# Expert tiles that join the block pipeline of the feed-forward part, from three tables

## The chip, the cores and the metric

The kernel runs on one core of a Trainium2 chip. Its time is device microseconds of that core. In the profile, PE is TensorE's matrix multiply and PEld its weight load, DVE is VectorE, ACT is ScalarE, POOL is GpSimd, and SP is SyncE, which issues most loads. All arithmetic is in 32-bit floats unless noted.

## The reference, cut to what matters

The layer works on x of 8 sequences of 512 tokens with 256 features. It has windowed causal self-attention with 16 heads, then cross-attention to 64 context rows per sequence, then a feed-forward part. The change is in the feed-forward part only, which is (with S = 512 positions and B = 8 sequences in the role of the batch):

```
xn  = layer_norm(x)
y   = layer_norm1(attention over the 8 sequences of a position(xn) + xn)
idx = argmax(y @ Wg.T)                       # one of E = 8 experts for each of 4096 tokens
for e in range(E):
    h   = relu(y @ W1[e] + b1[e])            # 256 -> 1024
    out = out + (idx == e) * (h @ W2[e] + b2[e])   # 1024 -> 256
result = x + layer_norm2(y + out)
```

The reference computes all experts for all tokens and masks. The kernel sorts the tokens by expert and computes for each only its own.

## The kernel before, in words

There are three stages. The first (lines 194 to 690) does both attentions, sequence by sequence; its output goes to a DRAM tensor x2d. The change does not touch it.

**The block stage** (lines 702 to 954). The 4096 tokens are split into NBLK = 8 blocks of 512 (64 positions x 8 sequences), each of NG = 4 groups of 128. For a block n there are a load (`block_load`, SyncE, into a buffer y that holds for each token two times 256 numbers and its token number), `block_start` (layer norm, transposes on PE, products for queries, keys and values), four `group` works (scores with a mask, maxima on DVE, exponentials on ACT, reciprocal on DVE, scaling of the softmax weights s by it on POOL at line 826, transposes on PE at line 831, product with the values at 838, output product at line 849), and a `block_end` (layer norm on DVE with a power on POOL, transposes at line 862, router product at line 868, arg max, the running count of tokens per expert `seens`, the rank of each token within its expert, and four scatters at line 928). A scatter is an indirect DMA on POOL's queue which writes 128 rows of 513 numbers to the DRAM tensor rows_d. Row e * 4096 + rank belongs to the token with that rank in expert e.

**The table** (lines 968 to 1025). When all 8 blocks are counted, a product with ones gives the number of tokens of each expert, and some twenty small DVE instructions make from them, for each of NT = 39 tiles: its expert (`eidx`), the row of rows_d for each of its 128 partitions (`srci`), and which of them are empty (`void`). 39 is the most that 4096 tokens in 8 experts can need when each expert's last tile may be partly filled.

**The tile stage** (lines 1027 to 1105). `expert_tile(i)` goes over six steps: SyncE reads the expert number and issues the loads of W1 (1 MB), b1 and b2, and POOL gathers the tile's rows from rows_d (line 1039); a step of nothing; transposes on PE (1055); 16 products of the hidden layer (1066, the profile counts two instructions for each) with the ReLU on ACT (1072) and DVE (1074); 8 products with W2 (1081, all of W2 lies in SBUF) and the layer norm's statistics (1084 to 1091); the norm's end and a scatter to the output (1095).

**What sets the order.** `in_steps` runs works as generators. A work has a start step; in each step every active work runs up to its next `yield`, in the order of its rank (PREFIX first, EXPS last), and among equals the latest begun first:

```
PREFIX, TURN, VALUES, SMALL, SCORES, OTHER, EXPS = range(7)
...
works.append((4 * n, block_start(n)))
for g in range(NG):
    works.append((4 * n + 6 + g, group(n, g)))
```

So block n's groups begin at steps 4n + 6 to 4n + 9, and its `block_end` at step 4n + 15, with scatters five and six steps later. `in_order` then fixes that order on PE, DVE, ACT and POOL: none of them may pass an instruction that waits. SyncE's queue is placed by the framework's scheduler. The framework also adds waits where a buffer is used again and where one DMA reads what another has written. For rows_d, the scatters are declared disjoint among themselves.

The tile stage is a second call of `in_steps`, with pools of its own (`ws`, `tp`, `mo`, `ps_f`, `ps_m3`), opened after the block stage's pools are closed.

Of the kernel before, what the change touches and what calls it, by code (L numbers as in the profile page):

```python
# [8 lines left out]
F32 = mybir.dt.float32  # L9
I32 = mybir.dt.int32  # L10
# [7 lines left out]
P = 128  # L18
# [8 lines left out]
NG = 4  # L27
# [5 lines left out]
NT = (B * S + E * (P - 1)) // P  # L33
ROW = 2 * D + 1
# [3 lines left out]
PREFIX, TURN, VALUES, SMALL, SCORES, OTHER, EXPS = range(7)  # L38
# [58 lines left out]
def decoder_kernel(ctx: ExitStack, tc: tile.TileContext, a: dict, out: bass.AP):  # L97
# [604 lines left out]
    with ExitStack() as p2:  # L702
# [5 lines left out]
        fy = p2.enter_context(tc.tile_pool(name="fy", bufs=7))  # L708
        state = [{} for _ in range(NBLK)]

        def block_load(n):

            state[n]["yr"] = yr = fy.tile([P, NG, ROW], F32, tag="y", name=f"y_{n}")
            for g in range(NG):
                p0 = (n * NG + g) * GP
                nc.sync.dma_start(yr[:, g, D : 2 * D], x2d[:, p0 : p0 + GP, :])
# [21 lines left out]
        def block_start(n):  # L738
# [21 lines left out]
            for hf in range(2):  # L760
# [7 lines left out]
                k = fx.tile([P, 512], F32, tag="k", bufs=4)  # L768
# [172 lines left out]

        block_load(1)
        works = [(9, expert_weights())]
        for n in range(NBLK):
            works.append((4 * n, block_start(n)))
            for g in range(NG):
                works.append((4 * n + 6 + g, group(n, g)))
            if n < NBLK - 1:
                works.append((4 * n + 15, block_end(n, 0, NG)))
            else:  # L950
                works.append((4 * n + 13, block_end(n, 0, NG // 2)))
                works.append((4 * n + 15, block_end(n, NG // 2, NG // 2)))
        with in_order(tc):
            in_steps(works)
    seen = seens[-1]

    ps_f = ctx.enter_context(tc.tile_pool(name="ps_f", bufs=4, space=PSUM))
    ps_m = ctx.enter_context(tc.tile_pool(name="ps_m3", bufs=4, space=PSUM))
    ws = ctx.enter_context(tc.tile_pool(name="ws", bufs=4))
    tp = ctx.enter_context(tc.tile_pool(name="tp", bufs=1))  # L960
    mo = ctx.enter_context(tc.tile_pool(name="mo", bufs=2))
    tb = []
    for i in range(7):
        tb.append(tp.tile([P, ROW], F32, name=f"tb{i}"))
        nc.gpsimd.memset(tb[i], 0.0)


    pn = ps_m.tile([P, E], F32, tag="m")
    nc.tensor.matmul(pn, ones, seen, start=True, stop=True)
    cnt = wp.tile([P, E], F32, name="cnt")  # L970
    nc.vector.tensor_copy(cnt, pn)

    def by_pairs(n, m, name):
        return wp.tile([P, n, m], F32, name=name)

    t8 = by_pairs(E, NGRP, "t8")
    nc.vector.tensor_tensor(
        t8,
        cnt.unsqueeze(2).to_broadcast([P, E, NGRP]),
        cst[:, C_128 : C_128 + NGRP].unsqueeze(1).to_broadcast([P, E, NGRP]),  # L980
        ALU.is_gt,
    )
    nt = wp.tile([P, E], F32, name="nt")
    nc.vector.tensor_reduce(nt, t8, AX.X, ALU.add)
    sc = by_pairs(E, E, "sc")
    nc.vector.tensor_tensor(
        sc,
        nt.unsqueeze(1).to_broadcast([P, E, E]),
        cst[:, C_SCAN : C_SCAN + E * E].rearrange("p (a b) -> p a b", b=E),
        ALU.mult,  # L990
    )
    first = wp.tile([P, E], F32, name="first")
    nc.vector.tensor_reduce(first, sc, AX.X, ALU.add)

    tiles = cst[:, C_TILE : C_TILE + NT].unsqueeze(2).to_broadcast([P, NT, E])
    begun = by_pairs(NT, E, "begun")
    nc.vector.tensor_tensor(begun, tiles, first.unsqueeze(1).to_broadcast([P, NT, E]), ALU.is_ge)
    ei = wp.tile([P, NT], F32, name="ei")
    nc.vector.tensor_reduce(ei, begun, AX.X, ALU.add)
    eidx = wp.tile([P, NT], I32, name="eidx")  # L1000
    nc.vector.tensor_scalar(eidx, ei, -1.0, None, ALU.add)


    oe = wp.tile([P, 2, 1 + E], F32, name="oe")
    nc.gpsimd.memset(oe, 0.0)
    nc.vector.scalar_tensor_tensor(
        oe[:, 0, 1:], first, -float(P), cst[:, C_E4 : C_E4 + E], ALU.mult, ALU.add
    )
    nc.vector.scalar_tensor_tensor(oe[:, 1, 1:], first, float(P), cnt, ALU.mult, ALU.add)
    od = wp.tile([P, 2, E], F32, name="od")  # L1010
    nc.vector.tensor_tensor(od, oe[:, :, 1:], oe[:, :, :E], ALU.subtract)
    ob = wp.tile([P, 2, NT, E], F32, name="ob")
    ov = wp.tile([P, 2, NT], F32, name="ov")
    for i in range(2):
        nc.vector.tensor_tensor(
            ob[:, i], begun, od[:, i].unsqueeze(1).to_broadcast([P, NT, E]), ALU.mult
        )
    nc.vector.tensor_reduce(ov, ob, AX.X, ALU.add)
    pos = cst[:, C_POS : C_POS + NT]
    void = wp.tile([P, NT], F32, name="void")  # L1020
    nc.vector.tensor_tensor(void, pos, ov[:, 1], ALU.is_ge)
    src = wp.tile([P, NT], F32, name="src")
    nc.vector.tensor_tensor(src, ov[:, 0], pos, ALU.add)
    srci = wp.tile([P, NT], I32, name="srci")
    nc.vector.scalar_tensor_tensor(srci, void, float(FAR), src, ALU.mult, ALU.add)

    def expert_tile(i):

        e_sp = nc.sync.value_load(eidx[0:1, i : i + 1], min_val=0, max_val=E - 1)
# [179 lines left out]
```

## Time and profile before

| | us |
|---|---|
| three runs | 1229.08, 1237.77, 1235.94 |
| median of the runs | 1235.94 |
| the profiled execution, its own time | 1234.02 |
| its span, from the first to the last instruction | 1232.3 |
| PE busy in the span | 1098.1 (89%) |
| PE's weight loads busy | 792.0 (64%) |
| DVE busy | 713.4 (58%) |
| ACT busy | 581.2 (47%) |
| POOL busy | 501.1 (41%) |
| first PE product of the block stage | 678.2 |
| last PE product of the block stage and table | 908.8 |
| first hidden layer of the tile stage | 932.5 |
| last PE product | 1217.4 |

The times of single instructions below come from the profiled execution and count from its span's start. A group's line has the source line, engine, operation, output<-input by tile name, how often, and busy time. In a timeline line the first number is the start, the second the duration, both in us, and the bracket at the end says how long the engine was idle before it and what released it. The granted clock is the share of full speed that PE was given. Matmuls are pipelined, so pieces of PE's timeline overlap by about 0.1 us.

### The profile page before, as it was taken

How to read it: one execution, taken by the hardware profiler on the slowest of the kernel's cores; microseconds unless marked ns; L12 is line 12 of the kernel's file. 1: busy time of each engine (PE TensorE's matmuls, PEld its weight loads, DVE VectorE, ACT ScalarE, POOL GpSimd, SP SyncE). 2: the span in 40 equal slices, each digit the busy share in tenths (PEclk: the TensorE clock that was granted, in tenths of full speed). 3: DMA queues.
4: the chain of work that ended last, by engine and by line, in shares of the span. 5: the costliest groups of instructions: out<-in, count | busy, mean ns of one | idle time of the engine just before them, and what ended most of it. 6: DMA issues, size and time to landing. Idle time of an engine off the chain costs nothing.

```text
span 1232.3 us, 24539 instructions
## 1 busy us (share of the span) xinstructions
PE 1098.1 (89%) x8901; PEld 792.0 (64%) x8901; DVE 713.4 (58%) x1804; ACT 581.2 (47%) x2040; POOL 501.1 (41%) x578
## 2 busy tenths in 40 slices
PE   6798998999989998998973999999737999999995
PEld 3455666566655665656542566676527999999994
DVE  2947768486684857857542436765652454545453
ACT  2866659576586766768510465555401111111110
POOL 2242424314343233522410333454353555555553
PEclk9997999999999999999997899999867999999998
DMA  5000001010010101000003840111066566666630
GB/s 190 1 1 5 6 1 45 1 39 6 18 27 2 44 1 36 10 1 27 2 18 98 242 131 2 52 53 52 35 170 243 196 206 218 223 208 208 217 126 9
DMA packets 60727, 97.66 MB, mean 79 GB/s; under 512 B 15930, under 2 KB 43965, under 8 KB 60608
## 3 DMA queue, kind: packets, MB, share of 16 engines
q1 hardware_dynamic: 53056, 75.08, 19.3%
q0 software_dynamic: 7552, 21.02, 5.0%
q8 instruction: 72, 1.18, 0.4%
q14 instruction: 47, 0.39, 0.1%
HBM read 81.12 MB, written 17.71 MB: 80 GB/s over the span
## 4 chain that ended last, share of the span: by engine, by line
PE 70%; DVE 15%; ACT 5%; issue 3%; POOL 3%; DMA 2%; SPq 0%; POOLq 0%; DVEq 0%
PE ps L183 12%; PE ps L1066 12%; PE ps L188 11%; PE ps L1081 11%; ACT s L447 3%; DVE nm L443 2%; PE sc L400 2%; DVE s L427 2%; PE xav L634 2%; DVE nm L576 2%; PE pt L476 2%; PE ps L802 2%; PE ps L177 2%; PE xk L598 2%; PE av L505 1%
## 5 line engine op out<-in xcount | busy, mean ns | idle before, releaser
L447 ACT ACTIVATE s<-s,nm 128x144 f32<-128x144 f32 (+1 forms) x512 | 203.4, 408 | 10.9 <-DVE nm L443 10.9
L1072 ACT ACTIVATE h<-ps,b 128x128 f32<-128x128 f32 x156 | 44.5, 368 | 261.3 <-issue 225.8
L1066 PE MATMUL ps<-tT,w 128*128 128x128 f32 x1248 | 148.3, 278 | 1.7 <-DMA b<-in_b 1.7
L1066 PEld LDWEIGHTS ps<-tT,w 128*128 128x128 f32 x1248 | 145.0, 195 | 2.1 <-issue 2.1
L1081 PE MATMUL ps<-w,h 128*128 x624 | 141.0, 379 | 0.0
L482 POOL TENSOR_TENSOR pc<-pT,cst 128x512 f32<-128x512 f32 x96 | 123.2, 1304 | 25.8 <-DVE pT L478 25.4
L1081 PEld LDWEIGHTS ps<-w,h 128*128 128x128 f32 x624 | 115.8, 191 | 14.0
L447 ACT ACTIVATION_READ_ACCUMULATOR s<-s,nm 128x1 f32 x512 | 100.8, 197 | 0.0
L458 POOL COPY rx<-s 128x128 f32<-128x128 f32 x48 | 14.6, 305 | 192.6 <-ACT s L447 192.6
L443 DVE TENSOR_REDUCE nm<-s 128x8 f32<-128x1152 f32 (+1 forms) x64 | 84.5, 1320 | 13.2 <-POOL s L436 9.4
L400 PE MATMUL sc<-kz,qT 32*128 32x512 f32 (+1 forms) x512 | 76.0, 603 | 4.1 <-DVE s L419 3.0
L427 DVE COPY_PREDICATED s<-upto_q,sc 128x512 f32<-128x512 int32 x96 | 64.6, 726 | 24.6 <-ACT s L426 24.6
L476 PE MATMUL pt<-cst,s 128*128 128x128 f32 x512 | 72.6, 282 | 2.6 <-ACT pT L480 1.1
L1074 DVE TENSOR_SCALAR h<-ps,b 128x128 f32<-128x128 f32 x156 | 43.9, 344 | 51.8 <-ACT h L1072 40.7
L156 POOL TENSOR_TENSOR rs<-rs,nhalf 128x4 f32<-128x4 f32 (+1 forms) x33 | 33.7, 1021 | 95.1 <-DVE rs L155 94.8
L476 PEld LDWEIGHTS pt<-cst,s 128*128 128x128 f32 x512 | 60.4, 145 | 15.5 <-issue 7.2
L426 ACT COPY s<-sc 128x512 f32<-128x512 f32 x96 | 51.6, 590 | 38.3 <-PE sc L400 38.3
L1091 POOL TENSOR_TENSOR rs<-rs,nhalf 128x1 f32<-128x1 f32 x39 | 26.5, 680 | 106.1 <-DVE rs L1090 91.3
L1084 DVE TENSOR_TENSOR r<-ps,r 128x256 f32<-128x256 f32 x39 | 16.6, 425 | 90.1 <-PE ps L1081 87.8
L183 PE MATMUL ps<-fxT,w_fwqkv 128*128 128x512 f32 x128 | 60.9, 621 | 0.0
L826 POOL TENSOR_TENSOR s<-s,sm 128x512 f32<-128x512 f32 x32 | 33.3, 1042 | 65.3 <-DVE sm L825 65.1
L461 DVE RECIPROCAL rc<-sm 128x8 f32<-128x8 f32 x64 | 12.6, 197 | 80.0 <-ACT s L447 80.0
(198 smaller groups left out, 2341.3 us busy)
## 6 DMA issues: line engine op xcount, KB each, us to landing
w<-in_W SPq DMA_DIRECT2D x47, 1024.0 KB
b<-in_b SPq DMA_DIRECT2D x39, 128.0 KB
xb<-in_x SPq DMA_DIRECT2D x8, 512.0 KB
x2d<-xb SPq DMA_DIRECT2D x8, 512.0 KB
y<-x2d SPq DMA_DIRECT2D x32, 128.0 KB
mi<-in_mask SPq DMA_DIRECT2D x8, 128.0 KB
mj<-in_maskT SPq DMA_DIRECT2D x8, 128.0 KB
w_wqkv<-in_wqkv SPq DMA_DIRECT2D x1, 768.0 KB
```

The lines of the kernel that those rows point to most:

```text
L183: nc.tensor.matmul(ps, w[:, k, o0 : o0 + P], xT[:, k, :], start=k == 0, stop=k == 1)
L188: nc.tensor.matmul(ps, xT[:, k, t0 : t0 + P], w[:, k, o0 : o0 + D], start=k == 0, stop=k == 1)
L400: nc.tensor.matmul(ps[j // 2][:, j % 2].rearrange("p r w k -> p r (w k)"), qT[rows[j], hf, q0 : q0 + P], kz[rows[j], hf, :, q0 + P - nw * ...
L426: nc.scalar.copy(s4, ps[jj][:, :, :, 0, :])
L427: nc.vector.copy_predicated(s4, upto_q.unsqueeze(1).unsqueeze(1).to_broadcast([P, 2, 2, P]), ps[jj][:, :, :, 1, :],)
L443: nc.vector.tensor_reduce(nm, s[:, :, :nk], AX.X, ALU.max, negate=True)
L447: nc.scalar.activation(s[:, h, :nk], s[:, h, :nk], AF.Exp, bias=nm[:, h : h + 1], accum_out=sm[:, h : h + 1],)
L476: nc.tensor.transpose(pt[:, h, :], s[:, 4 * jj + h, :P], ident)
L482: nc.gpsimd.tensor_tensor(pc[:, hs, :], pT[:, hs, :], upto_k.unsqueeze(1).to_broadcast([P, 4, P]), ALU.mult,)
L1066: nc.tensor.matmul(ps[:, j, :], w1[:, k, f * P : (f + 1) * P], tT[:, k, :], start=k == 0, stop=k == 1)
L1072: nc.scalar.activation(h[:, f, :], ps[:, j, :], AF.Relu, bias=b1[:, f : f + 1])
L1081: nc.tensor.matmul(ps, h[:, f, :], w2[:, bass.ds(e_pe, 1), f, :].rearrange("p o d -> p (o d)"), start=f == 0, stop=f == NFC - 1)
```

## The change

The tile stage's loop is gone. Its works are put into the list of the block stage, so that there is one call of `in_steps`.

- **Three tables.** Table 0 is made at step 32, when blocks 0 to 3 are counted; it holds 9 tiles, the number of full tiles that 2048 tokens in 8 experts always contain. Table 1, at step 40, is made from six blocks (17 tiles in all, so 8 more), and table 2, at step 48, from all eight (the other 22). Tables 0 and 1 hold only whole tiles, so they have no `void`. `taken` keeps how many tiles each expert has given; the next table starts behind them. In sum there are 39 tiles as before.
- **Tiles in the pipeline.** Tile i starts at step 34 + i with rank PREFIX. Its gather is issued in its first step; its loads one step later (rank LOADS, a new last rank); transposes one step later (TURN); hidden layer, output product and end follow in one step each.
- **Buffers.** The block buffers y have six names, y0 to y5, instead of seven turns of one name. W1 of a tile goes into y2 to y4 for the first seven tiles, and into y2 to y5 later. Tile rows live in three buffers of their own and four of the keys' buffers; b2 in the queries' buffers, r in the values', the hidden layer h in the buffers of xn and xT by turns. PSUM pools are the block stage's: the hidden layer takes one of the two large buffers that the scores use, instead of two of four smaller ones.
- The last block's `block_end` is one piece of four groups again, instead of two of two groups.

```
+NB1, NB2 = 4, 6
+NT1, NT2 = (-(-(n * NG * P - E * (P - 1)) // P) for n in (NB1, NB2))
-PREFIX, TURN, VALUES, SMALL, SCORES, OTHER, EXPS = range(7)
+PREFIX, TURN, VALUES, SMALL, SCORES, OTHER, EXPS, LOADS = range(8)
...
-            state[n]["yr"] = yr = fy.tile([P, NG, ROW], F32, tag="y", name=f"y_{n}")
+            state[n]["yr"] = yr = fy.tile([P, NG, ROW], F32, tag=f"y{n % 6}", name=f"y_{n}")
...
-                k = fx.tile([P, 512], F32, tag="k", bufs=4)
+                k = fx.tile([P, ROW], F32, tag="k", bufs=4, name="k")[:, :512]
...
+        def table(name, cnt, op, n, base, ends):
...
+            nc.vector.tensor_tensor(
+                t8,
+                cnt.unsqueeze(2).to_broadcast([P, E, NGRP]),
+                cst[:, C_128 : C_128 + NGRP].unsqueeze(1).to_broadcast([P, E, NGRP]),
+                op,
+            )
...
+            tables.append((eidx, srci, void))
+            return first, nt
+
+        def counts():
+            ps = ps_m.tile([P, E], F32, tag="m")
+            nc.tensor.matmul(ps, ones, seens[-1], start=True, stop=True)
+            return ps
...
+        def make_table(name, n, whole):
+
+            rest = wp.tile([P, E], F32, name=name + "rest")
+            nc.vector.scalar_tensor_tensor(rest, taken, -float(P), counts(), ALU.mult, ALU.add)
+            base = wp.tile([P, E], F32, name=name + "base")
+            nc.vector.scalar_tensor_tensor(
+                base, taken, float(P), cst[:, C_E4 : C_E4 + E], ALU.mult, ALU.add
+            )
+            if whole:
+                nc.vector.tensor_scalar(rest, rest, float(1 - P), None, ALU.add)
+            first, nt = table(name, rest, ALU.is_gt, n, base, not whole)
+            if whole:
+
+                take = wp.tile([P, E], F32, name=name + "take")
+                nc.vector.tensor_scalar(take, first, -1.0, float(n), ALU.mult, ALU.add)
+                nc.vector.scalar_tensor_tensor(take, take, 0.0, nt, ALU.max, ALU.min)
+                nc.vector.tensor_tensor(taken, taken, take, ALU.add)
+            yield
...
+        def expert_tile(i):
+
+
+            at = [0, NT1, NT2]
+            k = sum(i >= n for n in at) - 1
+            (eidx, srci, void), j = tables[k], i - at[k]
+            if i < 7:
+                if i < 3:
+                    t = tp.tile([P, ROW], F32, name=f"tb{i}")
+                else:
+                    t = fx.tile([P, ROW], F32, tag="k", bufs=4, name=f"tb{i}")
+                nc.gpsimd.memset(t, 0.0)
+                tb.append(t)
+            t = tb[i % 7]
+            nc.gpsimd.indirect_dma_start(
+                out=t.bitcast(I32),
+                out_offset=None,
+                in_=rows_d,
+                in_offset=bass.IndirectOffsetOnAxis(ap=srci[:, j : j + 1], axis=0),
+                bounds_check=E * B * S - 1,
+                oob_is_err=False,
+            )
+            yield LOADS
+            e_sp = nc.sync.value_load(eidx[0:1, j : j + 1], min_val=0, max_val=E - 1)
+            w1 = fy.tile([P, NG, ROW], F32, tag=f"y{2 + i % 3 if i < 7 else (2, 5, 3, 4)[i % 4 - 2]}", name=f"w1_{i}")
...
+            b2 = fx.tile([P, 512], F32, tag="q", bufs=4, name=f"b2_{i}")[:, :D]
...
+            yield TURN
...
+                nc.tensor.transpose(pt[:, k, :], t[:, k * P : (k + 1) * P], ident)
+            tT = fs.tile([P, 2, P], F32, tag="tT", bufs=2, name="tT")
+            nc.vector.tensor_copy(tT, pt)
+            yield EXPS
+            e_pe = nc.tensor.value_load(eidx[0:1, j : j + 1], min_val=0, max_val=E - 1)
+            h = fx.tile([P, NG, D], F32, tag=("xn", "xT")[i % 2], bufs=1, name=f"h_{i}")
+            h = h.rearrange("p g d -> p (g d)").rearrange("p (f t) -> p f t", t=P)
+            ps = ps_a.tile([P, 2, 512], F32, tag="a", name="hps")
...
+            r = fx.tile([P, 2, D], F32, tag="v", bufs=4, name=f"r_{i}")[:, 0]
+            nc.gpsimd.tensor_tensor(r, t[:, :D], b2, ALU.add)
+            nc.gpsimd.tensor_tensor(t[:, D : 2 * D], t[:, D : 2 * D], be2, ALU.add)
+            yield EXPS
...
+            nc.gpsimd.tensor_tensor(rs, rs, nhalf[:, :1], ALU.pow)
+            yield
...
-            if n < NBLK - 1:
-                works.append((4 * n + 15, block_end(n, 0, NG)))
-            else:
-                works.append((4 * n + 13, block_end(n, 0, NG // 2)))
-                works.append((4 * n + 15, block_end(n, NG // 2, NG // 2)))
+            works.append((4 * n + 15, block_end(n, 0, NG)))
+        for k, (nb, n) in enumerate(((NB1, NT1), (NB2, NT2 - NT1), (NBLK, NT - NT2))):
+            works.append((4 * nb + 16, make_table(f"t{k}", n, nb < NBLK)))
+        for i in range(NT):
+            works.append((4 * NB1 + 18 + i, expert_tile(i), PREFIX))
         with in_order(tc):
             in_steps(works)
...
-    with in_order(tc):
-        in_steps([(i, expert_tile(i)) for i in range(NT)])
```

## The prediction

> **What bounds the kernel now.** I read the page's busy slices first. TensorE (PE) is at nine tenths or more nearly everywhere, with two dips: one before the block stage (slices 20 to 22), one before the tile stage (slices 28 to 30).
>
> ```profile
> PE   6798998999989998998973999999737999999995
> PEclk9997999999999999999997899999867999999998
> ```
>
> The slices are 30.8 us long. The granted clock sinks with the second dip. Then I asked for each engine's busy time in the stages around that dip; the first number is the stage's length, then PE, its weight loads, VectorE (DVE), ScalarE (ACT), GpSimd (POOL), the clock, and the DMA engines' busy share.
>
> ```profile
> 857.90:867.90 10.00, 10.00 (x98) 7.37 (x96) 5.63 (x25) 7.25 (x31) 3.17 (x4) 1.00 0.08 28
> 867.90:908.80 40.90, 28.17 (x188) 19.34 (x187) 28.40 (x113) 11.59 (x37) 19.75 (x20) 0.81 0.21 78
> 908.80:932.50 23.70, 1.38 (x4) 0.59 (x5) 6.03 (x23) 0.00 (x0) 13.82 (x19) 0.50 0.98 273
> 939.80:1217.40 277.60, 277.60 (x1905) 259.56 (x1904) 135.50 (x453) 43.34 (x152) 151.83 (x183) 1.00 0.57 192
> ```
>
> Up to 867.9 PE is full with blocks, from 939.8 to 1217.4 with tiles, at full clock. Between lie the drain of the last blocks (40.9 us with 28.17 us of PE work, much of it at a reduced clock) and the start of the tiles (23.7 us with almost none). The chain that ended last says what fills the start:
>
> ```profile
> 913.22 9.97 DMA w<-in_W
> ...
> 924.90 7.61 DMA b<-in_b
> 932.52 6.25 PE ps L1066 x32
> ...
> 938.99 3.57 PE ps L1066 x32
> 942.57 3.46 PE ps L1081 x16
> ```
>
> The first weights leave only after the table is made; the first tile's hidden layer takes 6.25 us instead of 3.57, the clock being down. A tile in steady state costs PE 0.22 + 3.57 + 3.46 = 7.25 us.
>
> **What the change takes away.** It still runs 39 tiles (9 + 8 + 22), so PE's work stays: 39 x 7.25 = 282.8 us of tiles, and of blocks after 867.9 the pieces of PE's timeline, taken at the length they have at full clock, some 24 us. Together 307 us. Before, PE needs 867.9 to 1217.4 = 349.5 us for them. At best 42.7 us go. The tail after PE's last product, 1217.4 to the 1234.0 us of the profiled execution, is the same three tile steps and exit in both.
>
> In steady state both kernels keep PE on its own chain: transposes, hidden layer, output, with weights asked for one tile's turn after another and four weight buffers (three for the first seven tiles). I put 0 on the new buffer names there: the cover is the 14 us between a weight buffer's release and its need, against a 1 MB load whose burst lasts some 5.5 us in the tile stage. Without the cover it would be 5.5 us less the remaining lead per tile. The expert number of table two is read on SyncE ahead of tile 6's weights, that of table three after tile 15's; both tables are made well before those weights are due, so again 0; a table that came a step late would delay all loads queued behind the reading.
>
> **What it puts in: tables.** Table code now runs three times on VectorE; by the one-time rows (0.16 to 0.48 us each) about 18 instructions, 3.5 us each for the first two, 5 us for the third. VectorE is 56% busy at the first, with waits of 1 to 2 us between its pieces; I count 1.0 us in all.
>
> **What it puts in: GpSimd's waits.** This is the step that decides. In the built order of the changed kernel, every scatter of a block waits until the latest gathers from rows_d have landed, and every gather after a scatter waits until that scatter has landed: the row store is one tensor for this purpose. The waits stand in GpSimd's queue, and behind them are queued the scaling of the softmax weights (L826), for which PE waits in the next step, the powers, the residual adds and the next gathers. Each of blocks 4 to 7 ends with gather, scatter, scatter, gather, scatter, scatter, gather: four round trips. The landing times:
>
> ```profile
> tb<-rows_d,srci POOLq DMA_INDIRECT x39, 5.7
> ...
> rows_d<-y,sloti POOLq DMA_INDIRECT x32, 5.1
> ```
>
> One by one, scatters take 3.7 to 5.5 us while the DMA engines are quiet, and 7.6 to 10.5 us in the burst at 908 to 922; gathers 5.1 to 6.5 us under the tile stage's traffic. [...] I take the rows: 5.3 us for a scatter from its issue, 5.6 us for a gather.
>
> GpSimd's timeline gives the places:
>
> ```profile
> 856.99 0.97 POOL L928 DMA_INDIRECT rows_d<-y,sloti  x1 [0.30 <-issue]
> 859.09 1.03 POOL L826 TENSOR_TENSOR s<-s,sm 128x512 f32<-128x512 f32 x1 [1.14 <-DVE sm L825]
> ...
> 874.72 1.06 POOL L928 DMA_INDIRECT rows_d<-y,sloti  x1 [4.99 <-DVE sm L825]
> ...
> 922.27 1.05 POOL L1039 DMA_INDIRECT tb<-rows_d,srci  x1 [6.42 <-DMA rows_d<-y,sloti]
> ```
>
> Walking the new queue from there:
> - Gather 0 stands ahead of the scaling at 859.09 and waits for the scatter of 856.99: 856.99 + 4.9 = 862; gather 1.05 and scaling 1.05 end at 864.2 instead of 860.1. PE wanted it at 861.5: 2.8 us.
> - The shift pushes block 5's normalisation on VectorE; PE waits 0.5 and 1.4 us.
> - Block 4's first scatters wait for gather 2 (871 + 5.6 = 876.6) and for their slots (877.8), and are out at 880.3; gather 3 waits for the second of them (879.3 + 5.3 = 884.6); the scaling behind it ends at 886.7. PE, with the first tile's hidden layer done, is there at 882.6: about 4.2 us.
> - The other two scatters wait for gather 3 (890.2), gather 4 for them (896.8), the scaling ends at 898.9 against PE's 897.3: 1.6 us. Tile 2's weights go into block 4's buffer, free at 896.8; landed near 903 against 901.5: 2 us with the queue's delay.
> - From there a step has 7.25 us of tile beside at most 3 us of block, and GpSimd's own work is some 4.2 us. Its waits for blocks 5 and 6 (about 12 us each block) fit: transposes want a gather two steps later. For block 7 with 8 us steps I find 2 us at tile 16.
>
> Sum: 1.0 + 2.8 + 0.5 + 1.4 + 4.2 + 1.6 + 2 + 2 = 15.5 us.
>
> **The clock after such waits.** PE's timeline shows the price of one:
>
> ```profile
> 860.57 1.13 PE L188 MATMUL ps<-w_fwo,oT 128*128 128x256 f32 x4
> ...
> 878.18 0.66 PE L831 MATMUL pt<-cst,s 128*128 128x128 f32 x4 [3.14 <-POOL s L826]
> ...
> 880.17 2.08 PE L188 MATMUL ps<-w_fwo,oT 128*128 128x256 f32 x4
> 882.04 1.06 PE L831 MATMUL pt<-cst,s 128*128 128x128 f32 x4
> ```
>
> After idling 3.14 us, four products take 2.08 instead of 1.03 to 1.13 us and four transposes 1.06 instead of 0.60: some 1.5 us lost. [...] I charge the 2.8, the 4.2 and the pair after it: 4 us. ScalarE's exponentials (2.4 us a group) share the two large PSUM buffers with the hidden layer; bounds 0 (they end while PE does the step's small products) to 1 us in each of five steps; nearest is the first, ScalarE being 58% busy. Below nothing is excluded, as this is a buffer shared by more users. The largest unknown is the landing under mixed traffic: at 3.7 and 5.1 us the stalls fall from 15.5 to about 5, at 6.5 for both they rise to about 30.
>
> Forecast: 42.7 - 15.5 - 4 = 23 us off. Profiled execution 1234.0 - 23 = 1211; the median of the runs shown is 1.9 us above the profiled one, so 1213.
>
> **The rivals.**
> - *The gap closes nearly whole.* For it: PE was full until 867.9, and in the tile stage GpSimd is busy 151.83 of 277.60 us. Against it: the 4.99 and 6.42 us waits above. Losses of 5 us: 1235.9 - 38 = 1198.
> - *The round trips eat the gain.* Scatters under tile traffic land in 7 to 8 us. Eight scatter waits by 2.5 us and eight gather waits by 0.5 us more make 24 us, of which slack hides a few: gain near 3, 1233.
> - *Slower: GpSimd becomes the bound of the mixed stretch.* The place is the four round trips of blocks 4 to 7. At the 10.5 us measured in the burst for a scatter and 6.5 us for a gather, a block's four trips take 34 us and GpSimd's own work in those four steps about 17 us: 51 us against 38 us of PE. Four blocks: 52 us lost, the clock 4 more, against 42.7 gained: 13 us slower, 1249. It turns at a mean landing of about 8 us for both kinds. Against it: 10.5 us was eight scatters queued with 4 MB of weights.
> - *It does not overlap.* If the tiles waited for the last block, we would stay at 1236; the order shows tile 0 between block 7's groups, so I give it no chance of its own.
>
> **How the numbers follow.** Forecast 0.62 (own range 1203 to 1223), gap closed 0.14, eaten 0.14, slower 0.10. A measurement of this kernel tells about 1% (12 us) from no change. Faster by over 1% (below 1223.6): nearly all of the first and the second, 0.74; slower by over 1% 0.09; between 0.17. Range 1197 to 1231: from the closed gap to the upper part of the eaten one.
>
> **What would show it.** No stage with an empty PE near 909 to 932, the clock never at 0.50 there; first hidden layer near 880, last near 1192 to 1196. Right: waits of GpSimd's gathers and scatters on DMA, 16 of them, some 3 to 5 us each, and PE waiting for the softmax scaling two to four times. Wrong: tile transposes that wait for gathers throughout tiles 5 to 20 (the slower rival), or scatters landing under 4 us with PE full (the closed gap). A tile step of more than 7.25 us after the blocks, or loads waiting on SyncE for a table, would break the zeros.

## The result, and the profile after

| | before | after |
|---|---|---|
| median of the runs compared, us | 1234.07 | 1215.64 |
| lowest and highest, four runs each, us | 1229.08 to 1237.77 | 1214.40 to 1219.89 |
| the profiled execution's own time, us | 1234.02 | 1219.89 |
| its span, us | 1232.3 | 1218.1 |
| first PE product of the block stage | 678.2 | 681.4 |
| product that counts block 4's tokens (L908 before, L911 after; step 36) | 867.7 | 881.1 |
| last PE product ends | 1217.4 | 1204.3 |

The median of before holds a fourth run, 1232.19 us. The ratio of the times is 0.9859, with a 95% interval of 0.9814 to 0.9905: faster by 1.4%, 18.4 us in the medians. The forecast was 1213 us, in a range of 1197 to 1231.

Three times of PE divide the profiled executions in a useful way: its first product of the block stage, the product that counts block 4's tokens (the expectations below call it block 4's router product; here it is the count product), and the end of its last product. What is new in the first of these stretches is table 0, gathers 0 to 2, the weight loads of tiles 0 and 1, and tile 0's transposes (0.38 us of PE); in the second lies everything else of the tiles. The times are read off PE's timeline: 867.7 - 678.2 = 189.5 us and 1217.4 - 867.7 = 349.7 us before; 199.7 and 323.2 us after. So the tiles' part is 26.5 us shorter, and the start of the mixed stretch 10.2 us longer: 16.3 us gained of the 42.7 us that PE's gap held. (In this execution the block stage also began 3.2 us later; the profiles of all kernels below begin it between 675.7 and 681.0, before at 678.2, so this is the first stage's own variation. The profiled execution is also the slowest of the four.)

The busy slices of the changed kernel's page, to be read against those of before:

```profile
PE   6798998999989999899876699999789999999995
PEclk9997999999999999999987699999899989999998
```

Slices are counted from 0. The deep hole before the tile stage (7, 3, 7 at slices 28 to 30 before) is gone. A shallower one is left at slices 28 to 29, with a lower clock in slice 28, and in slice 32 the clock dips once more. The hole at slices 20 to 22, before the block stage, is the first stage's end, which the change does not touch. Asked stage by stage (length, then PE, its weight loads, DVE, ACT, POOL, the granted clock, the DMA engines' share, GB/s), the changed kernel answers:

```profile
867.00:872.20 5.20, 0.12 (x2) 0.00 (x1) 0.51 (x2) 0.00 (x0) 2.17 (x3) 0.71 0.29 85
872.20:876.00 3.80, 3.80 (x23) 2.50 (x24) 0.00 (x0) 2.12 (x9) 2.52 (x3) 0.50 0.89 333
...
889.00:896.90 7.90, 3.49 (x32) 3.25 (x30) 1.58 (x7) 1.14 (x4) 3.60 (x4) 0.98 0.22 77
896.90:901.00 4.10, 4.05 (x33) 2.90 (x34) 0.00 (x0) 2.37 (x10) 2.27 (x3) 0.63 0.29 108
901.00:930.00 29.00, 28.13 (x202) 25.11 (x200) 21.53 (x79) 6.00 (x19) 15.21 (x20) 1.00 0.73 244
...
986.00:997.00 11.00, 8.37 (x45) 7.97 (x44) 9.96 (x34) 0.07 (x1) 9.10 (x12) 0.69 0.74 236
...
1022.00:1032.00 10.00, 7.03 (x41) 6.64 (x41) 4.19 (x13) 1.01 (x4) 8.72 (x11) 0.83 0.86 285
1032.00:1204.30 172.30, 172.28 (x1175) 160.65 (x1174) 86.11 (x284) 26.45 (x93) 94.12 (x117) 1.00 0.55 177
```

From 901 us on PE is nearly full at full clock, but for two places. Each idle stretch is followed by one of reduced clock: 5 us without work and 3.8 us at 0.50, then 4.5 us and 4.1 us at 0.63, then 0.69 and 0.83 in windows that hold a 2.6 us wait and the hidden layer behind it. PE's timeline names who was waited for:

```profile
872.20 1.11 PE L834 MATMUL pt<-cst,s 128*128 128x128 f32 x4 [5.08 <-POOL s L829]
873.24 1.12 PE L841 MATMUL av<-pT,v 128*64 128x128 f32 x8
...
896.95 1.11 PE L834 MATMUL pt<-cst,s 128*128 128x128 f32 x4 [4.46 <-POOL s L829]
...
989.17 0.66 PE L1094 MATMUL pt<-cst,tb 128*128 128x128 f32 x2 [2.63 <-DMA tb<-rows_d,t1srci]
...
990.76 6.08 PE L1105 MATMUL hps<-tT,w 128*128 128x128 f32 x32
...
1024.65 0.41 PE L1094 MATMUL pt<-cst,tb 128*128 128x128 f32 x2 [2.57 <-DMA tb<-rows_d,t1srci]
1025.46 5.44 PE L1105 MATMUL hps<-tT,w 128*128 128x128 f32 x32 [0.40 <-issue]
...
1034.41 3.74 PE L1105 MATMUL hps<-tT,w 128*128 128x128 f32 x32
...
1041.66 3.74 PE L1105 MATMUL hps<-tT,w 128*128 128x128 f32 x32
```

Twice PE waits for the scaling of the softmax weights on POOL (`s`), twice for a gather's rows (`tb`, the last of table 1 at 1024.65). From 1034.41 to 1041.66 a tile takes 7.25 us, as before. POOL's timeline shows what stood ahead of the first two scalings:

```profile
859.73 1.06 POOL L931 DMA_INDIRECT rows_d<-y,sloti  x1 [9.12 <-DVE sm L828]
...
864.76 0.97 POOL L931 DMA_INDIRECT rows_d<-y,sloti  x1 [0.30 <-issue]
...
870.00 1.07 POOL L1067 DMA_INDIRECT tb<-rows_d,t0srci  x1 [3.72 <-DMA rows_d<-y,sloti]
871.10 1.05 POOL L829 TENSOR_TENSOR s<-s,sm 128x512 f32<-128x512 f32 x1
...
889.03 0.97 POOL L931 DMA_INDIRECT rows_d<-y,sloti  x1 [0.31 <-issue]
...
894.77 1.05 POOL L1067 DMA_INDIRECT tb<-rows_d,t0srci  x1 [4.23 <-DVE to L1087]
895.85 1.05 POOL L829 TENSOR_TENSOR s<-s,sm 128x512 f32<-128x512 f32 x1
```

Gather 0 leaves at 870.00, 5.24 us after the start of the scatter that it waits for, and the scaling is behind it in the queue. The same again at 889.03, 894.77 and 895.85. The scatters of block 3 themselves start late: block 4's norm and block 3's slots stand on DVE behind table 0, which fills 848.79 to 854.09. Its first and last piece, and block 3's slots:

```profile
848.79 0.16 DVE L1035 SCALAR_TENSOR_TENSOR t0rest<-taken,ps 128x8 f32<-128x8 f32 x1
...
853.92 0.17 DVE L1048 TENSOR_TENSOR taken<-taken,t0take 128x8 f32<-128x8 f32 x1
...
859.27 0.17 DVE L929 CAST sloti<-slot 128x4 int32<-128x4 f32 x1
```

### The profile page after: what moved, and what is told of

The parts are those of the page before. It is cut to its first block, busy times and chain, and to the rows that moved or that the text cites. A ratio compares the mean times of both kernels' runs of the same rounds, so it can differ in the third digit from the quotient of the medians.

```text
span 1218.1 us, 24488 instructions
## 1 busy us (share of the span) xinstructions
PE 1100.2 (90%) x8900; PEld 793.9 (65%) x8900; DVE 722.7 (59%) x1830; ACT 581.8 (48%) x2037; POOL 498.7 (41%) x580
## 4 chain that ended last, share of the span: by engine, by line
PE 64%; DVE 18%; ACT 8%; issue 3%; DMA 3%; POOL 3%; SPq 0%; POOLq 0%; DVEq 0%
PE ps L185 12%; PE ps L190 11%; PE hps L1105 9%; PE ps L1121 9%; ACT s L449 5%; PE sc L402 2%; DVE nm L445 2%; DVE s L429 2%; PE xav L636 2%; DVE nm L578 2%; PE ps L179 2%; DMA rows_d<-y,sloti 2%; PE av L507 2%; PE ps L805 1%; DVE kg L362 1%
## 5 line engine op out<-in xcount | busy, mean ns | idle before, releaser
L1110 ACT ACTIVATE h<-hps,b 128x128 f32<-128x128 f32 x156 | 44.6, 369 | 233.7 <-issue 188.6
L1105 PE MATMUL hps<-tT,w 128*128 128x128 f32 x1248 | 150.2, 280 | 0.7 <-issue 0.6
L1105 PEld LDWEIGHTS hps<-tT,w 128*128 128x128 f32 x1248 | 146.7, 196 | 2.0 <-issue 0.6
L1112 DVE TENSOR_SCALAR h<-hps,b 128x128 f32<-128x128 f32 x156 | 43.9, 344 | 65.0 <-ACT h L1110 58.0
L158 POOL TENSOR_TENSOR rs<-rs,nhalf 128x4 f32<-128x4 f32 x32 | 33.4, 1043 | 95.5 <-DVE rs L157 95.4
L185 PE MATMUL ps<-xT,w_wqkv 128*128 128x512 f32 x128 | 58.5, 599 | 0.0
L1139 POOL DMA_INDIRECT out<-r,to x39 | 39.8, 1020 | 29.5 <-DVE r L1138 13.4
```

Source lines behind the costliest of these rows:

```text
L185: nc.tensor.matmul(ps, w[:, k, o0 : o0 + P], xT[:, k, :], start=k == 0, stop=k == 1)
L1105: nc.tensor.matmul(ps[:, f, :], w1[:, k, f * P : (f + 1) * P], tT[:, k, :], start=k == 0, stop=k == 1)
L1110: nc.scalar.activation(h[:, f, :], ps[:, f, :], AF.Relu, bias=b1[:, f : f + 1])
```

## The experiments

The table has what the following sections argue from. The three right-hand columns are the two stretches named above and their sum, of one profiled execution each. The changed kernel, e1_views and e7_raw have the same start, and their first stretches agree within 0.4 us. In the kernels that start the tiles a step later with the gather behind the scaling (e8, e10, e11), PE waits for gather 0's rows just behind the count product, and in e3 much later: that wait is then part of the second stretch, and only the sum compares them fairly. Ratios are against the kernel before.

| kernel | median us | ratio and 95% interval | blocks' start to block 4's count product | from there to PE's end | sum |
|---|---|---|---|---|---|
| before | 1234.07 | | 189.5 | 349.7 | 539.2 |
| changed kernel | 1215.64 | 0.9859 (0.9814 to 0.9905) | 199.7 | 323.2 | 522.9 |
| e1_views | 1198.57 | 0.9707 (0.9680 to 0.9733) | 200.0 | 307.1 | 507.2 |
| e2_table17 | 1216.26 | 0.9846 (0.9818 to 0.9873) | 198.6 | 325.3 | 523.9 |
| e2_start19 | 1218.08 | 0.9894 (0.9840 to 0.9948) | 196.6 | 329.5 | 526.1 |
| e3_start26 | 1230.55 | 0.9968 (0.9954 to 0.9981) | 191.8 | 346.1 | 537.9 |
| e4_turn | 1216.62 | 0.9860 (0.9840 to 0.9880) | 201.7 | 324.6 | 526.3 |
| e5_views_turn | 1199.38 | 0.9721 (0.9699 to 0.9742) | 201.9 | 305.1 | 507.0 |
| e6_views_turn_t17 | 1198.41 | 0.9706 (0.9679 to 0.9732) | 201.4 | 304.8 | 506.1 |
| e7_raw | 1212.68 | 0.9843 (0.9818 to 0.9869) | 200.1 | 320.2 | 520.3 |
| e8_views_turn_s19 | 1194.32 | 0.9683 (0.9658 to 0.9709) | 191.9 | 309.7 | 501.6 |
| e9_views_s19 | 1199.74 | 0.9729 (0.9697 to 0.9761) | 198.1 | 308.3 | 506.4 |
| e10_all_t17 | 1191.32 | 0.9664 (0.9645 to 0.9684) | 190.1 | 310.3 | 500.4 |
| e11_turn_s19 | 1212.43 | 0.9849 (0.9822 to 0.9876) | 191.5 | 327.5 | 519.0 |

### The waits between scatters and gathers (e1_views)

The gathers get a view of rows_d of their own, which counts as disjoint from the scatters' views. The one dependence that the data has is put back by hand: the first gather of each table waits for the scatters of all blocks that the table counts; the later ones stand behind it in POOL's queue. All other waits between gathers and scatters are gone. Everything is still computed.

```
-    group_rows = dram_disjoint_views(rows_d, NGRP)
+    group_rows = dram_disjoint_views(rows_d, NGRP + 1)
...
-                in_=rows_d,
+                in_=group_rows[NGRP],
...
+            for sc_i in scatters[: NG * (NB1, NB2, NBLK)[k]] if j == 0 else ():
+                tc.add_manual_dep(
+                    ga_i.ins,
+                    sc_i.ins.name,
+                    mybir.DependencyInfo(mybir.DependencyClass.Sync, mybir.DependencyReason.DATA),
+                    reason="rows",
+                )
```

> The gathers read rows_d through a view of their own, and only the first gather of each table waits, for the scatters of the blocks that its table counts; the other waits between scatters and gathers are gone. Theory A (GpSimd's round trips on rows_d keep the gain below 42.7 us): the waits of PE for the scaling behind gather 3 (4.5 us) and for the gathers of two late tiles (2.6 us each) go, and with them some 5 us of reduced clock: 1215.6 - 12 to 15 = 1201 to 1204. Theory B (what is left of the loss lies in the tables on VectorE and at the start of the tiles, and the round trips are hidden): not more than 3 us less, 1213 to 1216.

Measured: 1198.57 us (1198.13 to 1199.45), 17 us under the changed kernel. From block 4's count product to PE's end it takes 307.1 us, which is what the prediction had worked out for PE's work alone (307). The stretches of its trace say the same, in the columns of before:

```profile
889.00:930.00 41.00, 39.99 (x300) 35.24 (x299) 28.20 (x105) 10.10 (x34) 25.13 (x31) 1.00 0.63 216
930.00:1030.00 100.00, 99.86 (x710) 93.38 (x709) 63.55 (x224) 16.43 (x56) 65.59 (x79) 1.00 0.81 250
1030.00:1183.00 153.00, 153.00 (x1044) 142.76 (x1042) 75.68 (x249) 23.96 (x84) 82.65 (x103) 1.00 0.53 168
```

PE has 99.86 us of work in the 100 where the changed kernel had waits of 2.6 us, at full clock. What follows: all of the 16 us lost after block 4's count product are the waits between scatters and gathers, with the clock behind them. DMA traffic, buffers, DVE or the shared PSUM are no bound there, PE being full. The gain is above the expected 12 to 15 us. The start is as long as in the changed kernel (200.0 us), so that is a second loss: PE still waits 4.79 us for the scaling behind gather 0. There one such wait is real: gather 0 does read what block 3's scatters write.

### Which of those waits (e7_raw)

As e1_views, but each gather waits for the last eight scatters issued before it; scatters do not wait for gathers.

```
+            for sc_i in scatters[-8:]:
+                tc.add_manual_dep(
+                    ga_i.ins,
+                    sc_i.ins.name,
+                    mybir.DependencyInfo(mybir.DependencyClass.Sync, mybir.DependencyReason.DATA),
+                    reason="rows",
+                )
```

> Gathers through a view of their own as in the first experiment, but every gather waits for the landing of the last scatters before it, as in the changed kernel; scatters no longer wait for gathers. It splits the 17 us that the views gave. If each wait counts alike, about half stays: 1206 to 1209. If the loss is the round trip, one wait after the other, slack hides the one kind that is left: 1199 to 1203. If only gathers' waits matter: 1213 to 1216.

Measured: 1212.68 us. Of the 17 us that the view gains, 14 are lost again. So the gathers' waits for scatters alone cost nearly all of it; the scatters' waits for gathers add some 3 us at most on top of them. What those would cost alone was not run. PE waits 4.86 us for the scaling at 892.92, behind a gather that stood 4.72 us in POOL's queue, and for the rows of two gathers at 1008.56 and 1018.75:

```profile
1008.56 0.41 PE L1103 MATMUL pt<-cst,tb 128*128 128x128 f32 x2 [1.94 <-DMA tb<-rows_d,t1srci]
1009.37 3.81 PE L1114 MATMUL hps<-tT,w 128*128 128x128 f32 x32 [0.40 <-DVE h L1121]
...
1018.75 0.41 PE L1103 MATMUL pt<-cst,tb 128*128 128x128 f32 x2 [2.11 <-DMA tb<-rows_d,t1srci]
1019.59 3.81 PE L1114 MATMUL hps<-tT,w 128*128 128x128 f32 x32 [0.44 <-DVE h L1121]
```

### No overlap with the groups (e3_start26)

The tiles start at step 42 instead of 34, when most of the blocks' groups are done.

```
-            works.append((4 * NB1 + 18 + i, expert_tile(i), PREFIX))
+            works.append((4 * NB1 + 26 + i, expert_tile(i), PREFIX))
```

> The tables stay, all tiles start eight steps later (42 in place of 34), behind the last groups, so that they lie beside the ends of blocks 6 and 7 only. If the gain comes from filling the drain of the last groups and the table's and first loads' gap, the second part stays: the gap of 23.7 us is filled, the drain of 40.9 us with its low clock comes back for the larger part: 1221 to 1228. If the gain is only the tables and loads ahead of time, it stays at 1214 to 1219.

Measured: 1230.55 us, ratio 0.9968 in a tight interval, 2.6 us above what was expected. The drain is back (346.1 us for the second stretch, PE waiting 3.08 us for a norm at 894.48 and 9.75 us for a gather's rows at 912.94). So the gain comes from the overlap of tiles with the last blocks' attention, and not from the three tables or from the joint pools as such. The run has a second use: table 0 is still made at step 32, but no gather follows for ten steps, and its start is 191.8 us. That puts table 0 by itself at 191.8 - 189.5 = 2.3 us, and leaves 7.9 of the changed kernel's 10.2 us for gather 0; its wait of 5.08 us and the 1.9 us of half clock behind it make 7.0 of them.

### The start: one thing at a time (e2_table17, e2_start19, e4_turn)

Three edits to the changed kernel: the tables one step later; the tiles one step later; the gather behind the step's scaling instead of ahead of it.

```
-            works.append((4 * nb + 16, make_table(f"t{k}", n, nb < NBLK)))
+            works.append((4 * nb + 17, make_table(f"t{k}", n, nb < NBLK)))
```
```
-            works.append((4 * NB1 + 18 + i, expert_tile(i), PREFIX))
+            works.append((4 * NB1 + 19 + i, expert_tile(i), PREFIX))
```
```
-            works.append((4 * NB1 + 18 + i, expert_tile(i), PREFIX))
+            works.append((4 * NB1 + 18 + i, expert_tile(i), TURN))
```

> Each table is made one step later (block 4n + 17 in place of 4n + 16), the tiles start as before. Table 0 then stands behind block 3's slots on VectorE, so that its last scatters leave some 4.6 us earlier and gather 0 with them. Theory B': the 5.1 us that PE waits behind gather 0, and the half clock after it (1.7 us), come from the table's place: 1215.6 - 4 to 7 = 1209 to 1212. Theory A': they come from the landing of the scatter alone, and the table's 5 us only move: 1214 to 1217.

> The tables stay, all tiles start one step later (35 in place of 34). Gather 0 then comes when block 3's scatters have landed. If PE is bound by its work wherever it does not wait, a later start costs nothing, and the 5.1 us behind gather 0 with its half clock go: 1209 to 1212. If PE starves without the tiles, a step of 7.25 us is lost in part: 1216 to 1221.

> The changed kernel with one edit: a tile's first step, its gather, has rank TURN in place of PREFIX, so that on GpSimd it stands behind the scaling of the softmax weights of the same step and no longer ahead of it. The waits between scatters and gathers stay. Theory C (at the start PE loses 5.1 us, and 1.7 us more at half clock, because the scaling is queued behind gather 0's wait): PE's wait at the start goes, but the waits of the next scatters and gathers stay and now stand ahead of the next step's scaling: 1209 to 1213. Rival (the order does not matter, as GpSimd's queue is as long in sum): 1214 to 1217.

Measured: 1216.26, 1218.08 (one of its four runs took 1229.31) and 1216.62 us. None gains. Each trace shows where it went.

- With the table later, block 3's last scatter starts at 856.29, but the gather behind it only at 863.41, 7.12 us later instead of 5.24. The 1 MB load of W1 needs only the table's expert numbers; it now goes out at 857.00, beside the scatter (in the changed kernel at 854.06, 10.7 us ahead of it). The start is 198.6 us.
- With the tiles later, the start is 3.1 us shorter (196.6), but the gathers meet other scatters: PE waits 7.79 us for the scaling at 886.29 and 6.33 us for a gather's rows at 1014.13, and the second stretch grows by 6.3 us.
- With the gather behind the scaling, the scaling is on time; now PE waits for the gather's rows, in its timeline

```profile
870.83 0.66 PE L1094 MATMUL pt<-cst,tb 128*128 128x128 f32 x2 [5.65 <-DMA tb<-rows_d,t0srci]
```

at the first transposes of tile 0, half a microsecond longer than for the scaling before.

### The same with the view (e5_views_turn, e6_views_turn_t17)

The later rank on top of the view, then the later tables on top of both.

> Views as in the first experiment and rank TURN for the gathers together. Theory C: what the views leave, some 10.5 us between the start of the blocks and block 4's router, falls to the 3 to 4 us that table 0 costs on VectorE: 1198.6 - 6 to 7 = 1191 to 1193. Rival (the 10.5 us are the table's): 1197 to 1199.

> Views, rank TURN, and each table one step later, behind the block's slots on VectorE. If the table ahead of block 4's norm is the rest of the loss at the start, 2 to 3 us go: 1188 to 1190. If it only moves, 1191 to 1193.

Measured: 1199.38 and 1198.41 us (1193.80 to 1202.67) against 1198.57 with the view alone: no gain, and starts of 201.9 and 201.4 us. PE waits 6.13 and 7.15 us for gather 0's rows. The theory of e5, that gather 0's place ahead of the scaling is what the start costs, fell with it and with e4_turn. So did that of e6, that the table is the rest: block 3's last scatter then starts at 860.28, but gather 0 only 9.36 us later. In e5_views_turn the last scatter of block 3 starts at 860.21, gather 0 at 865.21, and its rows are transposed on PE at 871.82:

```profile
860.21 0.97 POOL L932 DMA_INDIRECT rows_d<-y,sloti  x1 [0.30 <-PE av L842]
...
865.21 1.09 POOL L1069 DMA_INDIRECT tb<-rows_d,t0srci  x1 [2.49 <-DMA rows_d<-y,sloti]
...
871.82 0.66 PE L1103 MATMUL pt<-cst,tb 128*128 128x128 f32 x2 [6.13 <-DMA tb<-rows_d,t0srci]
```

That is a round trip of 11.6 us for data that PE wants at step 36. The two transfers follow each other whatever stands between them; here the order in the queue only decided whether the scaling or the rows came late.

### Room for the round trip (e8_views_turn_s19, e9_views_s19)

The view, with the tiles one step later; e8 has the gather behind the scaling as well.

```
-            works.append((4 * NB1 + 18 + i, expert_tile(i), TURN))
+            works.append((4 * NB1 + 19 + i, expert_tile(i), TURN))
```

> Own view of the row store for the gathers, gathers behind the scaling in their step, and tiles from step 35 instead of 34. Theory (the start's loss is one round trip, scatter of block 3 and then gather 0, which ends either in the scaling or in the tile's transposes, and one step of about 9 us more covers it): PE waits under 1.5 us for gather 0's rows or for the scaling in steps 35 to 37; block 4's router product comes 191 to 193 us after the blocks' first product instead of 200 to 202; time 1190 to 1193. Rival (the start is full of VectorE's work, or the later start gives back in the drain what it wins): PE waits 4 us and more elsewhere, 1197 to 1201.

> Own view, tiles from step 35, gathers still ahead of the scaling. If only the round trip counts, the scatter has landed a step earlier and the order behind the scaling is worth nothing: 1190 to 1194, as in the run with both. If gather 0's place ahead of the scaling still costs: a wait of 2 us for the scaling as in the run that started one step later without the view, 1194 to 1197. Rival of no gain: 1197 to 1201.

Measured: 1194.32 us (1193.50 to 1194.80) for e8, 1199.74 us for e9. PE's timelines at the start, of e8 and then of e9:

```profile
871.39 0.69 PE L1103 MATMUL pt<-cst,tb 128*128 128x128 f32 x2 [2.52 <-DMA tb<-rows_d,t0srci]
871.88 1.06 PE L835 MATMUL pt<-cst,s 128*128 128x128 f32 x4
873.66 1.12 PE L842 MATMUL av<-pT,v 128*64 128x128 f32 x8 [0.73 <-ACT pT L837]
```

```profile
868.38 1.12 PE L835 MATMUL pt<-cst,s 128*128 128x128 f32 x4 [2.35 <-POOL s L830]
...
872.17 2.07 PE L191 MATMUL ps<-w_fwo,oT 128*128 128x256 f32 x4
...
883.38 0.66 PE L835 MATMUL pt<-cst,s 128*128 128x128 f32 x4 [3.20 <-POOL s L830]
```

In e8 one wait of 2.52 us is left. Block 4's count product, now ahead of that wait, is at 191.9 us, as in the run without a gather there (191.8). The expectation is met there, but not in the wait (under 1.5 us) nor in the time, which is 1.3 us over its upper end. By the sums e8 gains 5.6 us on e1_views, by the medians 4.3. In e9 a step more is not enough: the scaling is late twice, first behind gather 0, which stood 3.10 us in POOL's queue, then behind block 4's scatters, which stood there 5.63 us until DVE came round to their slots. e9 ends where e1_views did, as its rival said. So the start's loss beyond the table is the round trip, and it takes both edits to hide the greater part of it: a step more between scatter and rows, and no scaling behind the waiting gather.

### What is left of the start, and the start without the view (e10_all_t17, e11_turn_s19)

e10 is e8 with tables one step later. e11 is e8 without the view, so with all waits between scatters and gathers as in the changed kernel.

> As the run with the view, the later rank and the start at step 35, and tables one step later. Theory (the 2.4 us that the start still loses are VectorE's table ahead of block 4's norm and block 3's slots): router product of block 4 at 189.5 to 191 us after the blocks' first product, wait for gather 0's rows gone, 1191 to 1193. Rival (the table's 5 us only stand in front of other work a step later, as in the run that moved the tables alone): 1194 to 1196.

> The changed kernel with gathers behind the scaling and tiles from step 35, without the view: scatters and gathers wait for each other as before. Theory (start and later round trips are two separate losses): the start loses 2 to 3 us instead of 10, the later waits stay at some 16 us: 1208 to 1211. Rival (the start's gain moves into later round trips, as with the later start alone): 1215 to 1218.

Measured: e10 1191.32 us (1190.49 to 1194.17), e11 1212.43 us. The count product of block 4 is at 190.1 us in e10: moving the table off block 3's slots is worth 1.8 us of the start, now that nothing else holds it, and 1.2 us in the sum. In medians e10 is 3 us under e8, but the two were timed against different runs of before and the intervals of their ratios overlap (0.9645 to 0.9684 against 0.9658 to 0.9709), so the table's worth is shown by the trace rather than by the time. The wait for gather 0's rows was expected to go; it is 3.51 us, longer than in e8:

```profile
857.35 0.97 POOL L932 DMA_INDIRECT rows_d<-y,sloti  x1 [0.30 <-issue]
...
867.11 1.09 POOL L1069 DMA_INDIRECT tb<-rows_d,t0srci  x1 [2.62 <-DMA rows_d<-y,sloti]
...
872.73 0.44 PE L1103 MATMUL pt<-cst,tb 128*128 128x128 f32 x2 [3.51 <-DMA tb<-rows_d,t0srci]
```

Counted from the blocks' start, the scatter leaves 4.3 us earlier than in e8, but gather 0 only 0.5 us earlier: the scatter now takes 9.8 us, where e8's gather left 5.9 us behind it. W1's load goes out at 857.70, beside it, as in e2_table17. The slices of e10:

```profile
PE   6798998999989999899987499999989999999995
PEclk9997999999999999999997699999989999999998
```

In e11 the count product is at 191.5 us, but gather 0's wait (2.03 us at 870.19, with four transposes in 1.06 instead of 0.60 us behind it) stands after it, so the second stretch, 327.5 us, is 4.3 us longer than in the changed kernel. The later waits, of 3.12, 2.98 and 3.40 us, sum to about what the changed kernel's three do (4.46, 2.63 and 2.57). By the sums e11 gains 3.9 us on the changed kernel, by the medians 3.2; the intervals of the two ratios overlap, so the time alone does not show it. It lies between the two expectations. The traces fit two separate losses, with some 4 us of the start's won.

e10_all_t17 is the fastest version that was run: 40.5 us under the kernel before (1231.86 us in the runs shared with it), and 24 us under the changed kernel by the medians. From the blocks' start to PE's end it takes 500.4 us against 539.2 before, so 38.8 of the 42.7 us are won.

## Why the prediction was right, point by point

The sign, the size within 3 us of the median, and the mechanism came out as put. The sum behind it was too kind by 7 us: of 42.7 us the forecast left 23, the profiled pair shows 16.3 between the blocks' start and PE's end, and the medians 18.4. That the median came so near is in part luck. The 1.9 us added for the median of three runs were gone with the fourth run (median 1234.07, profiled 1234.02); without them the forecast is 1211, 4.6 us low. And two terms that measured nothing (1.6 and 2 us) made up for part of those that were too small.

- **PE's work, 307 us.** Right: 307.1 us in e1_views, with PE full.
- **A tile step of 7.25 us, and the zeros.** Right. None of PE's waits in the changed kernel is for W1. SyncE does stand 6.8 us for table 1's expert numbers, ahead of tile 6's load, which the forecast had put at nothing; no PE wait comes of it. The zero does rest on its cover: in e4_turn, PE waits 3.75 us for W1 at 903.90, in e6_views_turn_t17 1.50 us at 905.38. The shared PSUM buffers cost nothing in e1_views, where PE is full (ScalarE was busier before the first of these steps than the 58% put for it: 7.25 of 10 us in the row shown).
- **Tables on DVE, 1.0 us.** Mis-sized: 2.3 us by e3_start26. The count of instructions was right and their mean too low. Table 0 takes 5.3 us (848.79 to 854.09), not 3.5; two of its pieces took 1.03 and 0.88 us. The forecast laid the instructions into the waits between VectorE's pieces; but they run in one block, ahead of block 3's slots, on which the scatters wait.
- **Gather 0 ahead of the scaling, 2.8 us, and block 5's normalisation behind it, 1.9 us.** Mis-sized. The wait for the scaling measured 5.08 us. The landing was near (5.24 us from the scatter's start to the gather's; the walk used 4.9). The scatter's start was wrong: walked from before's 856.99 without the table's delay. Counted from the blocks' start it is at 183.3 us instead of 178.8, so 4.6 us late, of which PE's own delay of 2.4 us behind the table takes off half: 2.8 + 4.6 + 0.3 - 2.4 = 5.3. Of the two waits behind it, put at 0.5 and 1.4 us, the trace lists none for the normalisation; PE waits 0.73, 0.85 and 0.73 us there for ACT, for the scaling and for ACT again.
- **The scaling behind gather 3, 4.2 us.** Right: 4.46 us at 896.95. Counted from the blocks' start, scatter and PE both come there some 6.6 us later than walked, so the difference held.
- **The scaling behind gather 4, 1.6 us; tile 2's W1, 2 us.** Both measured nothing. PE comes to those points later than walked; that the waits ahead had delayed it enough fits, but was not isolated.
- **Tile 16, 2 us.** Right in place and near in size: 2.57 us at 1024.65. The same round trip at tile 12 (989.17, 2.63 us) was not foreseen; the prediction had said that blocks 5 and 6 fit.
- **The clock, 4 us.** An estimate from one row of before (1.5 us lost after 3.14 us of idling), and mis-sized. After 5.08 us of idling PE has half clock (0.50) for 3.8 us, 1.9 us lost. After 4.46 us four transposes, the values' and the router's products take 1.11 + 1.12 + 1.05 instead of 0.60 + 0.66 + 0.64: 1.4 lost. After 2.63 and 2.57 us the hidden layers take 6.08 and 5.44 instead of 3.74: 2.3 and 1.7 lost, and the small products before the first some 0.8 more. In sum 8.1 us. The mechanism was charged to waits up to tile 2 only; it was dearer at the late tile steps, which have a whole hidden layer to run at the low clock. So of the 26.4 us lost (42.7 - 16.3), some 18 are stalls, against 15.5, and 8 are clock, against 4.
- **Landing times.** Right for scatters. In the eight pairs after 889 us of POOL's timeline in which a gather follows block 4's to 7's scatters, 4.65 to 5.87 us pass from the scatter's start to the gather's, median 5.5 (5.3 assumed). Where a scatter was released by a gather's landing, 3.62, 3.73, 5.55 and 6.61 us passed from the gather's start, against 5.6 assumed.
- **The signs.** GpSimd's timeline has 13 waits of a gather behind scatters or a scatter behind gathers, of 1.3 to 4.2 us, against 16 of 3 to 5; PE waits for the scaling three times (5.08, 0.85 and 4.46 us), within the two to four named. The first hidden layer is at 888.46, later than the 880 forecast, the last at 1193.64, as forecast. Between 909 and 932 PE is nearly full; the clock of 0.50 came at 872 instead.

The rivals. *Closing whole* is what e1_views comes to (1198.57, against the 1198 worked out): its price was right, and its condition is that the waits go, not that the landings are short. *Eaten* and *slower* needed scatters of 7 us and more under tile traffic; the changed kernel has none above 5.87 us. *No overlap*, put at 1236 and given no chance, has its nearest case in e3_start26 with 1230.55.

Not tried: gathers or scatters on another queue than POOL's, a table spread over several steps, and the later table with W1's first load held back from the scatter. So it is open what of e10's remaining 3.51 us could go.

## What to carry to other kernels

Where one queue issues dependent DMAs among compute instructions, count for each the instructions that stand behind its wait, and ask first whether the dependence is in the data or only in the tensor's name: a separate view for the readers, with the true dependences put back, was worth 17 us here, nearly as much as the whole change. A round trip through DRAM that is real needed a step of its own here; reordering around it only moved the wait to whoever was next. And where a run is divided at one instruction, check that an edit does not just move a wait across it: in e11 the later start did that with half of what it seemed to gain. And charge the clock where PE resumes with a long piece of work: a 2.6 us wait cost 4 to 6 us there.

## What the runs showed of the hardware

- **Reduced clock after idling.** At the tile steps PE's hidden layer took 5.41 to 6.26 us instead of 3.74 to 3.84 after idling 2.57 and 2.63 us in the changed kernel, 3.54 and 3.95 in e2_table17 and 6.33 in e2_start19, and 3.81 us after 1.94, 2.10 and 2.11 us (e7_raw's lines above; e3_start26). The clock granted in the changed kernel's two was 0.61 (990.76 to 996.80) and 0.69 (1025.46 to 1030.90), against 1.00 in an undisturbed one (1034.41 to 1038.15). At the block steps, with shorter pieces and gaps, slower pieces followed even 2.03 us (e11_turn_s19: four transposes in 1.06 instead of 0.60 us) and 2.35 us (e9: in 1.12). The length of one wait alone does not decide it, since 2.03 us was followed by it and 2.11 us was not.
- **A scatter beside a weight load.** From the start of block 3's last scatter to that of the gather waiting for it 5.24 us pass in the changed kernel, where W1's 1 MB load went out 10.7 us before the scatter. In e2_table17 it is 7.12 us and in e10_all_t17 9.8 us, with that load issued 0.7 and 0.35 us after the scatter; in e6_views_turn_t17, with the tables as late as in these two, it is 9.36 us. With the tables at the changed kernel's steps and tiles from step 34 or 35 (e1_views, e2_start19, e4_turn, e5_views_turn, e8, e9, e11) it is 4.95 to 5.93 us; in e8, which has the 5.93, the load goes out at 849.11, 10.7 us before the scatter. The cause was not isolated.
